# Two attention blocks on one core: N's and h's products alternate, ones product behind M5, sums of v and split of x reordered

## The chip, the cores and the metric

The kernel runs on one core of a Trainium2 chip. The metric is the device time of one execution in microseconds. Before the change it is 2845.95 us, the median of three runs (2843.32, 2845.95 and 2849.13). All data are fp32, in and out.

## What is computed

The input x is eight images of 512 channels and 64 x 64 positions. Two attention layers follow each other; the second one reads what the first one wrote.

```python
# layer 0
f = conv1x1(x, Wf, bf).reshape(b, c // K, h * w)
g = maxpool2x2(conv1x1(x, Wg, bg))
v = maxpool2x2(conv1x1(x, Wh, bh))
s = jnp.einsum('bcn,bcm->bnm', f, g)
beta = jax.nn.softmax(s, axis=-1)
o = jnp.einsum('bcm,bnm->bcn', v, beta).reshape(b, c // 2, h, w)
x = gamma * conv1x1(o, Wv, bv) + x
...
# layer 1
Qf = delu(Q).transpose(0, 2, 1)
Kf = delu(K)
KV = jnp.einsum('bmn,bcn->bmc', Kf, V)
norm = 1.0 / jnp.einsum('bnd,bd->bn', Qf, jnp.sum(Kf, axis=-1) + EPS)
attn = jnp.einsum('bnd,bdc,bn->bcn', Qf, KV, norm)
return x + gamma[0] * attn
```

Q, K and V are 1x1 convolutions of the first layer's result (below "x1"), and delu(x) = 10 relu(x) + exp(10 min(x, 0)).

## The kernel before

**Steps.** An image's 4096 positions are cut into 8 chunks of 512; there are 64 chunks, and `step(s)` (L747) does one chunk's worth of every stage, with the stages shifted against each other. In step s with image b = s // 8 and j = s % 8:

- stage A is for chunk a = s + 9: `a_fg` makes f and g, `a_h` makes h, its pooled form is v. Only 55 of the 64 steps with a chunk of their own (s = 0 to 54) have a stage A.
- E is for chunk s + 1: `weigh_two` makes scores and exponentials E, `sum_of_e` adds them up in r, `total` (L399) sums over partitions with a product by ones, `invert` (L403) takes the reciprocal, `look` (L408) notes two sums that show an overflow, `normalize_block` scales E.
- chunk s itself: `attend` (L437) multiplies v by E in seven products M1 to M7, `project` (L485) multiplies Wv by the result in N1 to N7 and adds it to x, `features` (L549) makes q and k from the new x1.
- chunk s - 1: `split_x`, `turn_halves` and `join_x` (L580 to L596) turn x1 over, `turn_k` turns k, `gather` (L613) makes G = k x1.
- image b - 1: `normalize` and `finish` (pairs of chunks, odd j) make the second layer's attention and add it to the output; `start_kb`, `turn_G` and `make_KV` come at j = 0.

**Seven products.** h, M and N are each a 2x2 block product done with seven products instead of eight. The operands' sums are made beforehand: of x by GpSimd in `sums_of_x` (t1 to t4 into `tha`, `thb`), of v by GpSimd in `sums_of_v` (S1 to S4, once an image), of E by VectorE in `sums_of_e` (T1 to T4), of o by VectorE in `to`. What a product gives is added where it belongs by VectorE. In N it is different: N5, N6 and N3 are accumulated into the PSUM bank of N1, and the bank is evicted between: `evict` (L512) copies it with ScalarE (L517, two instructions) into a scratch tile, and GpSimd adds that to a quarter of x (L520). The order is N1, evict (0,0), N6, evict (1,0), N5, evict (1,1), N3, and what is in the bank then is added by VectorE (`add_rest`, L525, L528). N2, N4 and N7 have banks of their own and are added to x by VectorE (`add`, L523).

**The order.** Nothing is reordered by a scheduler: within a step each piece of work is given a number, `at(t, fn)`, the list is sorted by it (L837), and each engine executes its own instructions in that order. The numbers are meant as microseconds but are no times; a wait is a semaphore between engines. The order of PE's work from N1 on, before the change, is N1 N2 N4 N6 N7 N5 H1 H2 N3 H3 H6 H5 H7 H4, then the turn of v (`a_turn`, pvT), then `features` (pk), then M1 of the next step.

**Buffers.** There are eight PSUM banks of 512 fp32 columns in one pool; `bank()` takes the one that was given back first. x1's chunk (`xb`) has a single buffer: its store, its splits and `features` must be done before the next chunk is loaded. The halves `w0` to `w3` and the turned halves `u0` to `u3` are single too.

**The turn of x1.** `split_x(s, k)` (L583) lets ScalarE part channel block k (128 channels) of x1 into upper and lower 16-bit halves; `turn_halves` turns them by a DMA that SP issues (L589); `join_x` (L596) lets ScalarE put the halves together in `xT`. Channel blocks 0 and 1 are x's quarters (0, .), which N1's last content finishes; blocks 2 and 3 are the quarters (1, .).

SP issues, in order, three transposes, the chunk's store (L534), the fourth transpose, stage A's next load (L200) and the next chunk's load (L205).

Of the kernel before, what the change touches and what calls it, by code (L numbers as in the profile page):

```python
# [38 lines left out]
ALU = mybir.AluOpType  # L39
# [10 lines left out]
def tile_two_attention_blocks(  # L50
# [21 lines left out]
    nc = tc.nc  # L72
# [4 lines left out]
    KT = C // P  # L77
# [86 lines left out]
    def run(ctx, general):  # L164
# [98 lines left out]
        def a_h(a, at, t_sums, t, t_pool):  # L263
            hk = KT // 2

            def sums_of_x():
                b11, b12, b21, b22 = (
                    x_a[a][:, bass.ts(i, hk), bass.ts(j, HN)] for i in range(2) for j in range(2)
                )
                ta, tb = blocks(f"tha_{a}", "T2"), blocks(f"thb_{a}", "T3")  # L270
                t1, t2, t3, t4 = (u[:, bass.ts(i, hk), :] for u in (ta, tb) for i in range(2))
                nc.gpsimd.tensor_tensor(t1, b12, b11, ALU.subtract)  # L272
                nc.gpsimd.tensor_tensor(t2, b22, t1, ALU.subtract)
                nc.gpsimd.tensor_tensor(t3, b22, b12, ALU.subtract)
                nc.gpsimd.tensor_tensor(t4, t2, b21, ALU.subtract)
                th[a] = {1: b11, 2: b21, 3: b22, 4: t4, 5: t1, 6: t2, 7: t3}

            m = {}

            def product(i):  # L280
                m[i] = bank(f"H{i}_{a}")[:, 0:HN]
                for k in range(hk):
                    nc.tensor.matmul(  # L283
                        m[i], w_h7[i][:, k, :], th[a][i][:, k, :], start=(k == 0), stop=(k == hk - 1)
                    )
                if i == 1:
                    u = m["m1"] = scratch(f"h1_{a}")
                    nc.scalar.copy(u[:, 0:HN], m[1])

            def out_1():  # L290
                h = hs[a] = blocks(f"h_{a}", "T4").rearrange("p (v j) n -> p v (j n)", v=VT)
                nc.vector.tensor_tensor(h[:, 0, 0:HN], m["m1"][:, 0:HN], m[2], ALU.add)

            def out_2():
                h, u, w = hs[a], m["m1"], scratch(f"h2_{a}")
                u2, u3 = u[:, HN:CH], w[:, 0:HN]
                nc.vector.tensor_tensor(u2, u[:, 0:HN], m[6], ALU.add)
                nc.vector.tensor_tensor(h[:, 0, HN:CH], u2, m[5], ALU.add)
                nc.vector.tensor_tensor(h[:, 0, HN:CH], h[:, 0, HN:CH], m[3], ALU.add)
                m["u2"], m["u3"] = u2, u3  # L300

            def out_3():
                h, u2, u3 = hs[a], m["u2"], m["u3"]
                nc.vector.tensor_tensor(u3, u2, m[7], ALU.add)
                nc.vector.tensor_tensor(h[:, 1, HN:CH], u3, m[5], ALU.add)
                nc.vector.tensor_tensor(h[:, 1, 0:HN], u3, m[4], ALU.subtract)

            def out_pool():
                vp = vps[a] = work.tile([P, VT, P], F32, tag="vp", name=f"vp_{a}")
                for v in range(VT):  # L310
                    pool(vp[:, v, :], hs[a][:, v, :])

            at(t_sums, sums_of_x)
            for i, d in ((1, -0.9), (2, 0.0), (3, 1.72), (6, 2.58), (5, 3.44), (7, 4.3), (4, 5.16)):
                at(t + d, product, i)
            at(t + 2.6, out_1)
            at(t + 4.4, out_2)
            at(t + 6.1, out_3)
            at(t_pool, out_pool)

        def bias_v(a):
# [11 lines left out]
        def sums_of_v(b):  # L333

            hm = MT // 2
            a11, a12, a21, a22 = (
                st[b]["vT"][:, bass.ts(j, hm), bass.ts(i, P)] for i in range(2) for j in range(2)
            )
            s1, s2, s3, s4 = (
                work1.tile([P, hm, P], F32, tag=f"S{i}", name=f"S{i}_{b}") for i in range(1, 5)  # L340
            )
            nc.gpsimd.tensor_tensor(s1, a21, a22, ALU.add)
            nc.gpsimd.tensor_tensor(s2, s1, a11, ALU.subtract)
            nc.gpsimd.tensor_tensor(s3, a11, a21, ALU.subtract)
            nc.gpsimd.tensor_tensor(s4, a12, s2, ALU.subtract)
            st[b]["v7"] = {1: a11, 2: a12, 3: s4, 4: a22, 5: s1, 6: s2, 7: s3}


# [136 lines left out]
        def project(s, at, t, t_store):  # L485

            m = {}

            def of_x(i, j):
                return x_b[s][:, 2 * i : 2 * i + 2, bass.ts(j, HN)]

            def product(i):
                o, u = os_[s], to[s]
                b = {
                    1: o[:, 0, 0:HN], 2: o[:, 1, 0:HN], 3: o[:, 1, HN:CH],
                    4: u[:, 3], 5: u[:, 0], 6: u[:, 1], 7: u[:, 2],  # L500
                }[i]
                more = i in (6, 5, 3)
                if not more:
                    m[i] = bank(f"N{i}_{s}").rearrange("p (k n) -> p k n", k=2)
                a = m[1] if more else m[i]
                for k in range(2):
                    nc.tensor.matmul(  # L507
                        a[:, k, :], w_v7[i][:, bass.ts(k, P)], b, start=not more and k == 0,
                        stop=True, skip_group_check=more or k > 0,
                    )  # L510

            def evict(ij):  # L512

                u = scratch(f"n{ij[0]}{ij[1]}_{s}").rearrange("p (k n) -> p k n", k=2)
                for k in range(2):
                    c = 2 * ij[0] + k
                    nc.scalar.activation(  # L517
                        u[:, k, :], m[1][:, k, :], AF.Identity, bias=gb_v0[:, c : c + 1]
                    )
                nc.gpsimd.tensor_tensor(of_x(*ij), of_x(*ij), u, ALU.add)  # L520

            def add(ij, i, op):
                nc.vector.tensor_tensor(of_x(*ij), of_x(*ij), m[i], op)  # L523

            def add_rest():  # L525
                for k in range(2):
                    x = x_b[s][:, k, HN:CH]
                    nc.vector.scalar_tensor_tensor(  # L528
                        x, m[1][:, k, :], gb_v0[:, k : k + 1], x, ALU.add, ALU.add
                    )  # L530

            def store():
                b, j = divmod(s, NCHUNK)
                nc.sync.dma_start(out=outr[b, :, :, bass.ts(j, CH)], in_=x_b[s])  # L534

            for n, i in enumerate((1, 2, 4, 6, 7, 5)):
                at(t + 0.86 * n, product, i)
            at(t + 6.88, product, 3)
            at(t + 0.9, evict, (0, 0))
            at(t + 3.45, evict, (1, 0))  # L540
            at(t + 5.2, evict, (1, 1))
            at(t + 3.8, add, (0, 0), 2, ALU.add)
            at(t + 5.6, add, (1, 0), 7, ALU.add)
            at(t + 6.3, add, (1, 0), 4, ALU.subtract)
            at(t + 7.0, add, (1, 1), 7, ALU.add)
            at(t + 7.7, add_rest)
            at(t_store, store)

        def features(s):  # L549
# [39 lines left out]
            nc.sync.dma_start_transpose(out=u, in_=halves[s, k].rearrange("p h n -> p (h n)"))  # L589

        def join_x(s, k):
            if k == 0:
                xTs[s] = turned.tile([P, NT, C], F32, tag="xT", name=f"xT_{s}")
            v = xTs[s].bitcast(U16).rearrange("p t (k c h) -> p k h t c", k=KT, h=2)
            u = turned_halves[s, k].rearrange("p (h t) c -> p h t c", h=2)
            nc.scalar.copy(v[:, k], u)  # L596
# [150 lines left out]
        def step(s):  # L747
# [27 lines left out]
            if 0 <= s - 1 < TOTAL:  # L775
                at(-0.5, features_exp, s - 1)
                at(-0.4, features_sum, s - 1)
                if s < TOTAL:
                    at(-0.45, join_x, s - 1, 1)
                    at(1.8, join_x, s - 1, 2)  # L780
                    at(2.3, join_x, s - 1, 3)
                at(3.6 if here else 0.2, turn_k, s - 1)
                if here:
                    gather(s - 1, at, 12.6, 13.5)
# [14 lines left out]
                finish(pair, (0, 1), at, 9.2)  # L799
                finish(pair, (2, 3), at, 10.9)  # L800
            if 0 <= a < TOTAL:
                a_h(a, at, 19.7, 30.8, 37.8)
                a_fg(a, at, 21.3)
            if 0 <= a - 1 < TOTAL:
                at(18.5, bias_v, a - 1)
# [3 lines left out]
            if after:  # L809
# [2 lines left out]
                at(7.5, weigh_two, n, 2)  # L812
                for m, t in ((2, 9.3), (4, 10.6), (6, 11.8), (8, 13.1)):
                    at(t, sum_of_e, n, m)
                at(16.1, total, n)
                at(17.0, invert, n)
                if not general:
                    at(21.5, look, n)
                at(24.3, normalize_block, n, 0, 1)
                at(26.0, normalize_block, n, 0, 0)  # L820
                at(27.3, normalize_block, n, 1, 1)
# [1 line left out]
                at(33.6, sums_of_e, n, 1)  # L823
                at(36.0, sums_of_e, n, 2)
            if here:
                project(s, at, 24.8, 36.0)
                at(37.0, features, s)
                if s < TOTAL - 1:
                    for k in range(KT):
                        at(32.9 + k, split_x, s, k)  # L830
                        at(33.0 + k, turn_halves, s, k)
                    at(37.3, join_x, s, 0)
                else:
                    for t in range(NT):
                        at(40.4 + t * 0.45, turn_x, s, t)
# [63 lines left out]
```

## Time and profile before

| what | before |
|---|---|
| median of three runs | 2845.95 us |
| the profiled execution, and its span | 2846.64 us, 2844.9 us |
| TensorE's mean granted clock | 0.988 |
| first N product of step 0 starts at | 143.14 us |
| from N1 to the next N1: odd j next, even j next | 43.49 us, 39.95 us (from the second image on) |
| the same where j = 0 leads on to j = 1 | 48.63 us |
| the eight images' part with all stages, 143.1 to 2460.8 | 2317.7 us |
| last eight steps and the end | 384.2 us |

A page describes one execution. PE is TensorE's matmul, PEld its weight load, DVE is VectorE, ACT is ScalarE, POOL is GpSimd, SP issues DMAs. In the list of waits a line reads: engine, tile and line that waited, "<-", the one that released it, then the total in us, the number of times, the longest. In a timeline a line is: start in us, duration in us, engine, line, operation, out<-in, shapes, count, and in brackets the idle time before it and what ended it. In the chain, a line is start, duration and what ran; "issue" is time in which nothing shown was waited for. The end of a matmul is modelled and reaches past the start of the next, so waits of PE are best read from one start to another.

### The profile page before, as it was taken

The numbers are of one execution on the slowest core, as the hardware profiler recorded it, in microseconds if no ns is written. First come the engines' busy times: TensorE is split into PE (matmuls) and PEld (weight loads), VectorE is DVE, ScalarE is ACT, GpSimd is POOL, SyncE is SP. The second block draws the span as 40 slices with busy tenths as digits, with TensorE's granted clock in tenths as the row PEclk, the third lists the DMA queues.
The fourth block names the chain that finished last, engine by engine and source line by source line (L and its number), as shares of the span: only waits on it lengthen the run. The fifth ranks groups of instructions, "written<-read, shape, count | busy, mean of one in ns | idle before, by whom it ended". The sixth has DMA issues, their size and how long they took to land.

```text
span 2844.9 us, 30593 instructions
## 1 busy us (share of the span) xinstructions
PE 2695.6 (95%) x10928; PEld 1810.9 (64%) x10928; DVE 2144.2 (75%) x2982; ACT 1516.6 (53%) x2629; POOL 709.6 (25%) x552
## 2 busy tenths in 40 slices
PE   8899999999999999999999999999999999989984
PEld 6566666666666666666766666666666666655551
DVE  4678778777787777877777877877878777787752
ACT  2255555556556556556556556456555556655542
POOL 4312222222321223222231222322222222211111
PEclk9999999999999999999999999999999999999996
DMA  4143244455454446454455454445544445544456
GB/s 155 36 119 91 88 119 133 97 140 148 115 137 119 108 129 163 98 139 120 118 133 148 106 131 131 120 120 148 118 120 135 118 118 148 133 101 110 112 138 119
DMA packets 394434, 346.96 MB, mean 122 GB/s; under 512 B 274592, under 2 KB 275104, under 8 KB 394272
## 3 DMA queue, kind: packets, MB, share of 16 engines
q1 hardware_dynamic: 371712, 275.82, 34.4%
q0 software_dynamic: 17408, 67.11, 12.7%
q10 hardware_dynamic: 5152, 1.97, 0.3%
q8 instruction: 89, 1.46, 0.2%
q14 instruction: 73, 0.60, 0.1%
HBM read 144.58 MB, written 134.22 MB: 98 GB/s over the span
## 4 chain that ended last, share of the span: by engine, by line
PE 71%; DVE 10%; ACT 8%; issue 4%; DMA 2%; POOL 2%; DVEq 0%; POOLq 0%; ACTq 0%
PE M L444 22%; PE N L507 11%; PE H L283 11%; PE fg L239 7%; PE pk L554 6%; PE s L354 5%; ACT n L517 3%; PE pa L732 3%; DVE r L394 3%; ACT E L358 3%; DMA u<-w 2%; PE tot L401 2%; PE pg L621 2%; DVE r L392 2%; ACT w L583 1%
## 5 line engine op out<-in xcount | busy, mean ns | idle before, releaser
L520 POOL TENSOR_TENSOR xb<-xb,n 128x512 f32<-128x512 f32 x192 | 244.5, 1274 | 596.4 <-ACT n L517 542.9
L444 PEld LDWEIGHTS M<-T,S 128*128 128x128 f32 x1536 | 287.3, 190 | 115.9 <-issue 30.7
L596 ACT COPY xT<-u 128x1024 uint16<-128x1024 uint16 x252 | 336.1, 1343 | 44.3 <-DMA u<-w 42.7
L444 PE MATMUL M<-T,S 128*128 128x256 f32 x1536 | 359.7, 384 | 0.0
L583 ACT COPY w<-xb 128x1024 uint16<-128x1024 uint16 x252 | 244.8, 1042 | 157.3 <-DVE xb L528 157.3
L517 ACT ACTIVATE n<-N,gb_v 128x256 f32<-128x256 f32 x384 | 161.5, 473 | 308.5 <-PE N L507 308.4
L420 DVE TENSOR_TENSOR E<-E,rtot 128x1024 f32<-128x1024 f32 x256 | 304.7, 1213 | 2.4 <-ACT tot L411 1.6
L358 ACT ACTIVATE E<-s 128x512 f32<-128x512 f32 x512 | 257.6, 626 | 42.6 <-PE s L354 42.1
L523 DVE TENSOR_TENSOR xb<-xb,N 128x512 f32<-128x512 f32 x256 | 175.1, 684 | 129.8 <-POOL xb L520 127.5
L507 PE MATMUL N<-to,w_v 128*128 128x256 f32 x1024 | 251.3, 389 | 15.0 <-ACT n L517 10.7
L392 DVE TENSOR_TENSOR r<-E 128x1024 f32<-128x1024 f32 x64 | 78.4, 1225 | 226.6 <-ACT E L358 226.6
L554 PE MATMUL pk<-xb,w_kqk 128*128 128x512 f32 x512 | 235.9, 604 | 10.5 <-DVE xb L528 10.5
L738 POOL DMA_DIRECT2D out_dram<-y x60 | 72.3, 1206 | 678.0 <-ACT y L735 675.8
L354 PE MATMUL s<-f,g 64*128 64x512 f32 x1024 | 239.7, 603 | 0.7 <-ACT kT L611 0.6
L406 DVE RECIPROCAL rtot<-tot 128x512 f32<-128x512 f32 x64 | 215.4, 3365 | 27.6 <-PE tot L401 27.6
L410 ACT ACTIVATE tot<-tot 128x512 f32<-128x512 f32 x64 | 37.2, 582 | 371.6 <-DVE rtot L406 364.5
L507 PEld LDWEIGHTS N<-to,w_v 128*128 128x128 f32 x1024 | 190.0, 191 | 66.5 <-ACT n L517 40.3
L444 PE MATMUL M<-E,vT 128*128 128x256 f32 x1024 | 231.6, 379 | 0.5 <-ACT vT L331 0.5
L272 POOL TENSOR_TENSOR tha<-xa 128x512 f32<-128x512 f32 x58 | 77.0, 1327 | 619.6 <-PE M L444 605.8
L444 PEld LDWEIGHTS M<-E,vT 128*128 128x128 f32 x1024 | 194.5, 190 | 54.0 <-issue 19.8
L507 PE MATMUL N<-o,w_v 128*128 128x256 f32 x768 | 195.1, 390 | 30.2 <-ACT n L517 27.3
L239 PE MATMUL fg<-xa,w_fg 128*128 128x512 f32 x464 | 210.6, 597 | 0.0
(129 smaller groups left out, 4647.0 us busy)
## 6 DMA issues: line engine op xcount, KB each, us to landing
xb<-in_x_dram SPq DMA_DIRECT2D x64, 1024.0 KB, 7.1
out_dram<-xb SPq DMA_DIRECT2D x64, 1024.0 KB, 5.0
out_dram<-y POOLq DMA_DIRECT2D x60, 1024.0 KB, 11.2
xa<-in_x_dram SPq DMA_DIRECT2D x58, 1024.0 KB, 6.6
w_v<-in_L_conv_wv_dram SPq DMA_DIRECT2D x8, 1024.0 KB, 9.1
x_early<-in_x_dram SPq DMA_DIRECT2D x6, 1024.0 KB, 5.4
out_dram<-y_late POOLq DMA_DIRECT2D x4, 1024.0 KB, 17.7
u<-w SPq DMA_TRANSPOSE x252, 3.3
```

The source lines that it names most:

```text
L239: nc.tensor.matmul(fg, w_fg[:, k, :], x_a[a][:, k, :], start=(k == 0), stop=(k == KT - 1))
L283: nc.tensor.matmul(m[i], w_h7[i][:, k, :], th[a][i][:, k, :], start=(k == 0), stop=(k == hk - 1))
L354: nc.tensor.matmul(sc[e], g[half(e), i, :], fs[s][half(e), :], start=True, stop=True)
L358: nc.scalar.activation(es[s][:, 2 * i + e, :], sc[e], AF.Exp)
L420: nc.vector.tensor_tensor(b, b, r, ALU.mult)
L444: nc.tensor.matmul(m[i], v7[i][:, k, :], te[s][i][:, k, :], start=(k == 0), stop=(k == hm - 1))
L507: nc.tensor.matmul(a[:, k, :], w_v7[i][:, bass.ts(k, P)], b, start=not more and k == 0, stop=True, skip_group_check=more or k > 0,)
L517: nc.scalar.activation(u[:, k, :], m[1][:, k, :], AF.Identity, bias=gb_v0[:, c : c + 1])
L520: nc.gpsimd.tensor_tensor(of_x(*ij), of_x(*ij), u, ALU.add)
L554: nc.tensor.matmul(pk, w_kqk[:, i, e * D : (e + 2) * D], x_b[s][:, i, :], start=(i == 0), stop=(i == KT - 1),)
L583: nc.scalar.copy(w, x_b[s][:, k, :].bitcast(U16).rearrange("p (n h) -> p h n", h=2))
L596: nc.scalar.copy(v[:, k], u)
```

## The change

1. In `project` and `a_h` the numbers of the products are set anew: on PE N1 N2 N4 N6 N7 H1 N5 H2 H3 N3 H6 H5 H7 H4. The copy of H1 (`copy_1`, before part of `product(1)`) gets a number of its own and comes behind the eviction (1,1) on ScalarE. The eviction (1,1), VectorE's add of N7 to (1,1), `add_rest` and h's sums get later numbers; their order on VectorE stays.
2. `total` comes behind M5 instead of before it in steps with even j; `invert` comes behind M7's place in all steps. In the one step that has E but no chunk of its own (s = -1), `total` comes behind fg, and `invert` and `look` behind it.
3. GpSimd makes S4 before S3. (M3 needs S4, M7 needs S3.)
4. The channel blocks of x1 are split, turned and joined in the order 2, 3, 0, 1 instead of 0, 1, 2, 3. The last split comes behind `a_turn`'s copy on ScalarE, and the store comes behind the fourth transpose on SP.

```diff
@@ a_h
-                if i == 1:
-                    u = m["m1"] = scratch(f"h1_{a}")
-                    nc.scalar.copy(u[:, 0:HN], m[1])
+
+            def copy_1():
+                u = m["m1"] = scratch(f"h1_{a}")
+                nc.scalar.copy(u[:, 0:HN], m[1])
...
-            for i, d in ((1, -0.9), (2, 0.0), (3, 1.72), (6, 2.58), (5, 3.44), (7, 4.3), (4, 5.16)):
-                at(t + d, product, i)
-            at(t + 2.6, out_1)
-            at(t + 4.4, out_2)
-            at(t + 6.1, out_3)
+            for i, n in ((1, 0), (2, 2), (3, 3), (6, 5), (5, 6), (7, 7), (4, 8)):
+                at(t + 0.86 * n, product, i)
+            at(t + 2.0, copy_1)
+            at(t + 4.45, out_1)
+            at(t + 6.1, out_2)
+            at(t + 7.8, out_3)
@@ sums_of_v
+            nc.gpsimd.tensor_tensor(s4, a12, s2, ALU.subtract)
             nc.gpsimd.tensor_tensor(s3, a11, a21, ALU.subtract)
-            nc.gpsimd.tensor_tensor(s4, a12, s2, ALU.subtract)
@@ project
-            for n, i in enumerate((1, 2, 4, 6, 7, 5)):
+            for i, n in ((1, 0), (2, 1), (4, 2), (6, 3), (7, 4), (5, 6), (3, 9)):
                 at(t + 0.86 * n, product, i)
-            at(t + 6.88, product, 3)
...
-            at(t + 5.2, evict, (1, 1))
+            at(t + 6.05, evict, (1, 1))
...
-            at(t + 7.0, add, (1, 1), 7, ALU.add)
-            at(t + 7.7, add_rest)
+            at(t + 8.2, add, (1, 1), 7, ALU.add)
+            at(t + 8.6, add_rest)
@@ join_x
-            if k == 0:
+            if s not in xTs:
@@ step
-                    at(-0.45, join_x, s - 1, 1)
-                    at(1.8, join_x, s - 1, 2)
-                    at(2.3, join_x, s - 1, 3)
+                    at(-0.45, join_x, s - 1, 3)
+                    at(1.8, join_x, s - 1, 0)
+                    at(2.3, join_x, s - 1, 1)
...
-                a_h(a, at, 19.7, 30.8, 37.8)
+                a_h(a, at, 19.7, 29.1, 37.8)
...
-                at(16.1, total, n)
-                at(17.0, invert, n)
+
+                at((17.85 if j % 2 == 0 else 16.1) if here else 21.4, total, n)
+                at(18.0 if here else 24.2, invert, n)
                 if not general:
-                    at(21.5, look, n)
+                    at(21.5 if here else 24.25, look, n)
...
-                project(s, at, 24.8, 36.0)
+                project(s, at, 24.8, 37.2)
...
-                    for k in range(KT):
-                        at(32.9 + k, split_x, s, k)
-                        at(33.0 + k, turn_halves, s, k)
-                    at(37.3, join_x, s, 0)
+
+                    for i, k in enumerate((2, 3, 0, 1)):
+                        at(33.8 + i, split_x, s, k)
+                        at(33.9 + i, turn_halves, s, k)
+                    at(38.3, join_x, s, 2)
```

## The prediction

> **What bounds the kernel now.** I read the page first (shares and slices), then the list of waits, then one step's timelines on PE, DVE, ACT and SP, then the chain of waits over the same step.
>
> ```profile
> PE 2695.6 (95%) x10928; PEld 1810.9 (64%) x10928; DVE 2144.2 (75%) x2982; ACT 1516.6 (53%) x2629; POOL 709.6 (25%) x552
> ...
> PEclk9999999999999999999999999999999999999996
> ```
>
> TensorE is 95% busy at full clock: it is the bound, and the work given to it does not change. So the change can gain at most TensorE's gaps, about 149 us, and must be judged gap by gap. The waits say what ends them:
>
> ```profile
> PE N L507 <- ACT n L517: 38.0, 70, 1.8
> PE tot L401 <- DVE r L397: 31.0, 37, 4.4
> ...
> PE M L444 <- POOL S L345: 5.6, 8, 3.5
> ```
>
> These three are named by the edits: N behind an eviction, `total` behind the sum of E, M3 behind GpSimd's sums of v. The chain shows the first one inside a step whose N1 starts at 1234.75:
>
> ```profile
> 1234.92 3.47 PE N L507 x16
> ...
> 1238.41 0.85 ACT n L517 x2
> 1239.26 0.04 issue
> 1239.30 1.13 PE N L507 x4
> 1240.43 0.88 PE H L283 x4
> ...
> 1241.60 0.85 ACT n L517 x2
> 1242.45 0.04 issue
> 1242.50 1.13 PE N L507 x4
> 1243.63 4.32 PE H L283 x20
> ```
>
> Read it as: N6 ends, ACT evicts the shared bank, N5 may start; N5 ends, ACT copies h1 and then evicts, N3 may start. Only one product (N7) covers the first eviction; H1 and H2 stand before the second, but H1's own copy goes ahead of it on ACT. The even steps' wait, on PE:
>
> ```profile
> 1306.14 1.99 PE L444 MATMUL M<-T,S 128*128 128x256 f32 x8
> 1308.65 1.10 PE L401 MATMUL tot<-r,ones 128*128 128x512 f32 x2 [0.52 <-DVE r L397]
> ```
>
> **What the Trainium skill says.** PSUM — Partial Sum Buffer, Terms: no two of TensorE, ScalarE and VectorE may access one bank of a partition in the same cycle. So accumulation into N1's bank must stand still while ACT reads it; the trace agrees (N5 starts 0.04 us after the 0.85 us eviction). TensorE: Matmul & The Clock Gate, Part 1: after an idle window of about 3.4 us the array falls to half clock. The trace agrees: after a gap of 4.36 us at 98.8 us, fg took 5.55 us instead of 3.60. GPSIMD Engine Reference, Specifications: GpSimd contends with VectorE instructions that read two SBUF inputs; at 114.3 us a sum of v took 2.36 us beside such work, against 1.26 for its neighbour.
>
> **Part 1, N and h alternate.** A product is four matmuls, 216 ns each (20 in 4.32 us above), so 0.864 us. Nine products from N1 to the end of N3 are 7.78 us; the PE timeline has H3 at 1243.46, 8.71 after N1. Waits: 0.93 us a step. New order: N1 N2 N4 N6 N7 H1 N5 H2 H3 N3 H6 H5 H7 H4. Relative to N1: N6's result could be evicted at 3.66 to 4.50 (as now), N5 comes at 5.18: cover 0.7. N5 ends 6.05; ACT, whose next instruction is now the eviction (h1's copy went behind it), evicts 6.25 to 7.09; N3 comes at 7.78: cover 0.7. Both waits go. The rest of the step: GpSimd's sum of quarter (1,1) 7.2 to 8.45 (1.27 us), DVE's N7 add at 8.5 (now 9.07), add_rest from 9.1 to 10.0 (now 9.7 to 10.6). pk, which needs add_rest, starts at 12.3 (now 13.25), so it has over 2 us. PSUM: each product still finds its bank freed by the same predecessor in issue order: H6 needs N2's add (4.2; H6 at 8.6), H7 needs h1's copy (7.4; H7 at 10.4), pvT and pk need the (1,1) adds: all early. H1 reads x alone, which is loaded. 55 steps have both families; the six with j = 0 after the first image are counted apart: 49 x 0.93 = 45.6 us.
>
> **Part 2, total behind M5 in even steps.** r is ready some 0.55 us after M6 has ended; M5 is 8 matmuls, 1.73 us, and needs only T1. So the wait (M6, begun at 1306.14, issues until 1307.87, tot starts at 1308.65; of these 0.78 a hand-over takes 0.1 anyway, and its second matmul is 0.08 late: 0.75) is covered with 1.0 us to spare. 21 even steps with j > 0 have it: 19 at 0.75, one near 1.0, one at 2.25 of which 0.6 stays: 17 us. Price: the reciprocal (3.37 us) starts as before in time, but PE is one product pair further, so DVE's chain to the normalizing comes up to 1.7 us later against N1: gp's reduce ends at N1 + 2.3, f's copies 3.65, and the (1,0) eviction, queued behind f on ACT, 3.7 to 4.5; N5 needs it at 5.18. The (1,0) adds move to 6.6 to 8.0, still ahead of the (1,1) add at 8.5. Cover 0.5 us; if it is gone each lost 0.1 us costs 2 us in all. Odd steps keep total's place; there pa (3.43 us) covers r already, except s = 1, 3, 5, 7, which keep their wait.
>
> **Part 3, steps with j = 0 (six).** There DVE is late (reciprocal of pd before that of tot), gp's reduce holds f, f holds the eviction, and N5 comes 1.94 us late (N1 at 1144.59 plus five products is 1148.91):
>
> ```profile
> 1150.85 1.13 PE L507 MATMUL N<-to,w_v 128*128 128x256 f32 x4 [1.78 <-ACT n L517]
> ```
>
> That time stays, since DVE's chain hangs on E. But H1 is already done by then, and N3 no longer waits: N5 at 1150.85, then seven products, pvT at 1157.9 instead of 1159.33: 1.46 us. S4 before S3 on GpSimd lets M3 go one sum (1.26 us) earlier; its wait is 0.43: gone, and M7, which now takes the last sum, comes some 15 us later (1256.18 and about 1271.4 in an odd step). 6 x 1.9 = 11.3 us.
>
> **Part 4, x's split.** ACT waits 2.50 us a step for add_rest before split 0. Channel blocks 2 and 3 of x need no add_rest, so split 2 starts at N1 + 9.2 (now 10.2). Split 1 is now behind vT's copy (pvT at 12.1): split 1 12.9 to 13.9, 0.2 earlier than the last split now, while PE is 0.93 earlier. But on SP:
>
> ```profile
> 1289.51 3.99 SPq L589 DMA_TRANSPOSE u<-w  x3
> 1293.59 0.53 SPq L534 DMA_DIRECT2D out_dram<-xb  x1
> 1294.22 1.99 SPq L589 DMA_TRANSPOSE u<-w  x1
> ```
>
> the fourth transpose is issued behind the store and 16.0 after N1; now it goes before it, at 14.5 (first three from 10.25, 1.4 us each, the fourth when split 1 is done). So it lands 1.5 us earlier, or more without the store's 1 MB ahead. Its join, which needed it 0.46 us sooner than it had it, then has room; kT, E and r move with PE. I count nothing, as E is bound by s. The store is issued 0.5 to 1 us later, as are xa's and xb's loads behind it; they have over 10 us (xb's load of 7.1 us is needed 23 us on).
>
> **Part 5, ends.** Before the first real step tot waits 4.36 us and then fg runs at half clock; now fg (3.43) fills that wait. But h's last products then need the banks of look and f, which hang on the reciprocal, so only about 1.5 us arrive at M1; S4's place gives M3 some 2 more (sums of 2.3 us under contention), and M5 before the next tot 1.7 and a shorter half-clock stretch: 6 us, between 3 and 9. In the last eight steps there is no h, N's waits stay; DVE's chain from tot to add_rest bounds even steps, fed by the last transpose, which lands some 1.2 us earlier: 4 us over four steps, between 0 and 8, since half-clock stretches may come or go there.
>
> **Sum**, against the profiled execution (span 2844.9, 2846.64 with what lies around it): 45.6 + 17 + 11.3 + 6 + 4 = 84, so 2762.7; the median shown is 0.7 below that execution: 2762.
>
> **Rivals.**
> Base, 78%: 2745 to 2780.
> A, the E chain does not keep up: split 1 behind vT's copy makes the last transpose late, E follows it instead of s. For: E starts 1.16 after s, with kT just done, in even steps now. Against: 1.5 us gained on SP, and M5 now forgives 1.0. It takes Part 2's 17 us and some of Part 1 in even steps (27 x 0.4): about 2790. 11%.
> B, the alternation does not free N, because ACT or a bank is not free where I think (f before the (1,0) eviction): half of Part 1 and Part 2 lost: 2795 to 2810. 5%.
> C, slower: the same transpose, landing really late. E stays with s while it lands by N1 + 20.8 (join 1.34 and kT 0.36 ahead of E at 22.5), 6.3 us after its issue. What is beyond holds PE in each of 55 steps, less some 1.1 us that M5 and the PSUM banks forgive (pa's first bank is free 1.3 us before pa, at 1260.2 against 1261.54). The gain is 1.5 a step, so C decides from about 9 us after issue; the longest I see is 6.62, at 1209.20 in the chain, behind a store. At 10 us it takes (3.7 - 1.1) x 55 = 143: 2905. 4%. The remaining 2% is no change.
>
> **Numbers.** Base and most of A and B lie in 2744 to 2800. Within 0.2% (5.7 us, about what a measurement of this kernel can tell from none) 2%, slower 4%, faster 94%.
>
> **What would show it.** After: N L507 <- ACT n L517 falls from 38 to some 15 us (j = 0 steps and the last eight), tot's wait from 31 to below 8, M <- POOL S near 0 in the steps; ACT w <- DVE xb shrinks; the step pair falls from 83.4 to about 80.8 us. Wrong, if N5 or N3 still waits in ordinary steps, if DVE's recip-to-gp stretch holds f, or if xT <- DMA u grows on ACT.

## The result, and the profile after

| what | before | after |
|---|---|---|
| median (four runs each) | 2847.52 us | 2773.56 us (2770.26 to 2776.02) |
| ratio, 95% interval | | 0.9742 [0.9725, 0.9759] |
| the profiled execution, and its span | 2846.64, 2844.9 us | 2770.26, 2768.5 us |
| first N product of step 0 | 143.14 us | 136.10 us |
| from there to step 55 | 2317.6 us | 2253.3 us |
| last eight steps and the end | 384.1 us | 379.1 us |

The change makes the kernel 2.6% faster. The span falls by 76.4 us: 7.0 at the start, 64.4 in the steps that have all stages, 5.0 at the end. The forecast had 6, 73.9 and 4. So the steps that have all stages are short by some ten microseconds, and the rest of this document looks for them.

First the page of the kernel after, its shares and its clock:

```profile
PE 2659.8 (96%) x10928; PEld 1820.9 (66%) x10928; DVE 2138.0 (77%) x2982; ACT 1511.6 (55%) x2629; POOL 712.4 (26%) x552
...
PEclk9999999999999999999999999999999999999996
```

The same 10928 matmuls, still at full clock to the eye. The slices of this row are 69 us wide, and that hides something, as will be seen. Then the list of waits on PE, after:

```profile
PE N L509 <- ACT n L519: 21.1, 15, 2.1
...
PE N L509 <- DVE o L476: 9.5, 10, 3.7
...
PE tot L403 <- DVE r L399: 5.7, 6, 2.9
```

The wait behind the eviction was there 70 times and is there 15 times; the wait of `total` was there 37 times and is there 6 times. But the first line is 21.1 us, not the forecast's 15, and its longest entry is 2.1 us where it had been 1.8. One step's PE timeline, in an ordinary even step whose N1 starts at 1197.40, shows what went right:

```profile
1197.40 1.89 PE L509 MATMUL N<-o,w_v 128*128 128x256 f32 x8
1199.13 2.75 PE L509 MATMUL N<-to,w_v 128*128 128x256 f32 x12
1201.72 1.03 PE L283 MATMUL H<-xa,w_h 128*128 128x256 f32 x4
1202.58 1.03 PE L509 MATMUL N<-to,w_v 128*128 128x256 f32 x4
1203.44 1.89 PE L283 MATMUL H<-xa,w_h 128*128 128x256 f32 x8
1205.17 1.03 PE L509 MATMUL N<-o,w_v 128*128 128x256 f32 x4
```

No line has a bracket: N1, N2, then N4, N6 and N7, H1, N5, H2 and H3, N3, without one wait. ScalarE in the same stretch:

```profile
1198.52 0.84 ACT L519 ACTIVATE n<-N,gb_v 128x256 f32<-128x256 f32 x2 [2.94 <-PE N L509]
1199.33 1.38 ACT L257 ACTIVATE f<-fg,b_fg 64x512 f32<-64x512 f32 x2
1201.05 0.84 ACT L519 ACTIVATE n<-N,gb_v 128x256 f32<-128x256 f32 x2 [0.35 <-PE N L509]
1203.64 0.84 ACT L519 ACTIVATE n<-N,gb_v 128x256 f32<-128x256 f32 x2 [1.75 <-PE N L509]
```

The second eviction ends at 1201.89 and N5 starts at 1202.58: 0.69 us of cover (the time by which an eviction is over before PE needs the bank). The third ends at 1204.48, N3 starts at 1205.17: again 0.69. The pair of steps fell from 83.44 to 80.81 us (42.55 + 38.26).

Now a step with j = 0, by engine, after. Three tiles matter: gT, a sum that VectorE makes from the turned G in two instructions; gp, VectorE's pooling of fg; and f, ScalarE's copy of fg, which waits for gp. Behind f in ScalarE's queue stands the eviction (1,0) that N5 waits for. First PE, then VectorE, GpSimd and ScalarE:

```profile
1116.55 1.89 PE L509 MATMUL N<-to,w_v 128*128 128x256 f32 x4 [2.08 <-ACT n L519]
1118.23 2.87 PE L283 MATMUL H<-xa,w_h 128*128 128x256 f32 x8
```

```profile
1103.92 3.36 DVE L408 RECIPROCAL rtot<-tot 128x512 f32<-128x512 f32 x1
...
1110.56 1.82 DVE L672 TENSOR_TENSOR gT<-g 128x256 f32<-128x256 f32 x2
...
1113.54 0.69 DVE L216 TENSOR_REDUCE gp<-fg 64x128 f32<-64x512 f32 x1
```

```profile
1110.44 1.32 POOL L522 TENSOR_TENSOR xb<-xb,n 128x512 f32<-128x512 f32 x1 [4.83 <-ACT n L519]
```

```profile
1114.27 1.38 ACT L257 ACTIVATE f<-fg,b_fg 64x512 f32<-64x512 f32 x2 [3.90 <-DVE gp L216]
```

And the two lines of the kernel before that belong beside them, VectorE's and GpSimd's:

```profile
1145.93 0.75 DVE L671 TENSOR_TENSOR gT<-g 128x256 f32<-128x256 f32 x2
```

```profile
1146.58 1.28 POOL L520 TENSOR_TENSOR xb<-xb,n 128x512 f32<-128x512 f32 x1 [4.83 <-ACT n L517]
```

Before, GpSimd's first addition began 0.1 us before the second gT instruction ended. After, PE reaches N1 earlier against VectorE's chain (N1 stands 4.54 us after the reciprocal of `total` began, before it was 5.29), so the eviction (0,0) and GpSimd's addition come earlier too, and the addition lies on top of gT: 0.75 us becomes 1.82. All of the growth is in the first of the two instructions:

```profile
1110.56 1.49 DVE L672 TENSOR_TENSOR gT<-g 128x256 f32<-128x256 f32 x1
```

It began 0.12 us after GpSimd's addition and was over 0.29 us after it; the second took 0.41 us as before. It is the same in all six j = 0 steps. From the reciprocal to the end of gp's reduction it is now 10.31 us, before it was 9.23. f, the eviction (1,0) and N5 hang on that, one behind the other, and N5 comes 1.08 us later against the reciprocal.

The same two lines of PE show a second loss. H2 and H3, eight matmuls, take 2.87 us where the ordinary step has 1.89, and N5's four take 1.68 from start to start instead of 0.86. Windows over four j = 0 steps (columns: stretch, length, PE busy and count, granted clock, DMA share, GB/s):

```profile
446.50:497.00 50.50, 48.22 (x187) 0.97 0.52 125
778.50:827.00 48.50, 46.23 (x186) 1.00 0.54 130
1108.50:1159.00 50.50, 48.22 (x187) 0.97 0.52 126
1440.00:1490.00 50.00, 47.72 (x192) 1.00 0.53 127
```

In the first and the third of them, and in the one at 1770, the clock fell to half for 3.4 us right behind the wait; in the other three it did not. From N1 to N1 these steps take 50.67 us and 49.00 us by turns, where the kernel before took 48.63.

### The profile page after: what moved, and what is told of

The parts are those of the page before. It is cut to its first block, busy times and chain, and to the rows that moved or that the text cites. A ratio compares the mean times of both kernels' runs of the same rounds, so it can differ in the third digit from the quotient of the medians.

```text
span 2768.5 us, 30622 instructions
## 1 busy us (share of the span) xinstructions
PE 2659.8 (96%) x10928; PEld 1820.9 (66%) x10928; DVE 2138.0 (77%) x2982; ACT 1511.6 (55%) x2629; POOL 712.4 (26%) x552
## 3 DMA queue, kind: packets, MB, share of 16 engines
q10 hardware_dynamic: 5152, 1.97, 0.3%
q8 instruction: 89, 1.46, 0.2%
## 4 chain that ended last, share of the span: by engine, by line
PE 86%; DVE 8%; issue 2%; ACT 2%; POOL 1%; DMA 0%; POOLq 0%; DVEq 0%; ACTq 0%
PE M L446 26%; PE H L283 14%; PE N L509 12%; PE pk L555 8%; PE s L356 7%; PE fg L239 7%; PE pg L622 4%; PE pa L733 3%; PE tot L403 2%; DVE rtot L408 1%; DVE r L396 1%; DVE E L422 1%; PE pkT L610 1%; ACT E L360 1%; PE pkv L686 1%
## 5 line engine op out<-in xcount | busy, mean ns | idle before, releaser
L597 ACT COPY xT<-u 128x1024 uint16<-128x1024 uint16 x252 | 329.3, 1340 | 9.9 <-DMA u<-w 9.0
L584 ACT COPY w<-xb 128x1024 uint16<-128x1024 uint16 x252 | 250.5, 1043 | 118.1 <-DVE xb L525 118.1
L509 PE MATMUL N<-to,w_v 128*128 128x256 f32 x1024 | 248.9, 387 | 15.3 <-ACT n L519 12.5
```

Of the source, the lines that this page charges most:

```text
L509: nc.tensor.matmul(a[:, k, :], w_v7[i][:, bass.ts(k, P)], b, start=not more and k == 0, stop=True, skip_group_check=more or k > 0,)
L584: nc.scalar.copy(w, x_b[s][:, k, :].bitcast(U16).rearrange("p (n h) -> p h n", h=2))
```

## Experiments

The theory: the shortfall sits in the six j = 0 steps. gT is slowed by GpSimd's addition, and the gap that follows sometimes costs the clock. Part 2 (PE ahead of VectorE by the time of M5's move) is what brings the two together. The rivals: Part 1 does not free what it should; the moved copy or the turn of x1 costs; the start gives less than it seems. In the profile of one run the start of step 0 is not a fine gauge: kernels whose start is the same as after's had it at 136.1, 137.95, 137.97 and 138.97 us.

**Part 1 alone.** Before, with the new places of N's and h's products and of h1's copy. The splits keep their old order, only 0.52 later.

```diff
-                    for k in range(KT):
-                        at(32.9 + k, split_x, s, k)
-                        at(33.0 + k, turn_halves, s, k)
+                    for k in range(KT):
+                        at(33.42 + k, split_x, s, k)
+                        at(33.52 + k, turn_halves, s, k)
```

> The alternation of N's and h's products alone, everything else as before. Theory (the waits of N5 and N3 go in 49 steps at 0.93 us; in the six steps with j = 0, N5's wait shrinks by one product, 0.86, and N3's 0.6 goes): 46 + 9 = 55 us, perhaps 3 to 6 of it given back because the last transposed half still comes behind the store and E starts a little late: about 2795, within 2788 to 2803. In the trace the step from N1 to N1 with odd j next falls from 43.49 to 42.55, and no half-clock stretch appears in the steps. Rival (a bank or ACT holds N): under 30 us gained, N5 or N3 still waiting.

Measured: 2804.03 us against 2850.83, ratio 0.9837 [0.982, 0.9853]. The ordinary steps fell by 0.94 each, and all six j = 0 steps from 48.63 to 47.17 us, by the 1.46 that the forecast had for them. gT stayed at 415 ns. So neither the alternation nor its count is what failed. The rest of the expectation was missed: 2804.03 against about 2795, above its range of 2788 to 2803. The profiled execution, 2810.53, is the longest of the four; in it five steps waited 2.09 to 2.23 us for `total`, where the kernel before has one such wait (2.09 us, at 1225.21 us), and behind three of the five the clock fell to half, which was not expected either. PE at one of them:

```profile
619.97 1.10 PE L403 MATMUL tot<-r,ones 128*128 128x512 f32 x2 [2.23 <-DVE r L399]
620.91 5.30 PE L446 MATMUL M<-T,S 128*128 128x256 f32 x16
```

The sixteen matmuls behind the gap take 3.62 us at full clock; here a part of them ran at half. ScalarE's fourth join had waited for its transpose:

```profile
610.71 1.34 ACT L597 COPY xT<-u 128x1024 uint16<-128x1024 uint16 x1 [1.74 <-DMA u<-w]
```

That transpose was issued at 604.81, behind the store. In all five steps the fourth join had waited so, by 1.19 to 1.74 us. With the old turn of x1 the late fourth transpose can come onto the path. That the faster steps are the reason why it does so more often is argued from one trace of each kernel, and not shown.

**Part 2 alone.**

```diff
-                at(16.1, total, n)
-                at(17.0, invert, n)
+                at(17.85 if here and j % 2 == 0 else 16.1, total, n)
+                at(18.0 if here else 17.0, invert, n)
```

> total behind M5 in even steps and invert behind M7, alone, and only in steps with a chunk of their own. My prediction's sum: 17 us from 21 even steps, 2 at s = 0, j = 0 unchanged: 2829. Theory formed from the changed kernel's trace: in j = 0 steps the VectorE chain is what N5 waits for, PE comes 0.75 us earlier to the eviction (0,0), so GpSimd's add of that quarter runs beside the sum gT, which reads two SBUF inputs: gT grows from 0.75 to some 1.8 us, N5's wait grows to about 3.8 us and most of these steps get a half-clock stretch of 3.4 us: 6 x (1.07 + up to 1.7) = 6 to 16 us back. So 2835 to 2843.

Measured: 2847.25 us against 2850.83, 0.998 [0.9969, 0.9991], above the expected 2835 to 2843. The eleven executions spread from 2837.97 to 2850.02 us; the fastest has a mean granted clock of 0.987, the slowest 0.982. The profiled one, 2842.79, is one of the faster ones. In its trace the even steps fell from 39.95 to 39.20, the 0.75 that was counted. And yet next to nothing is left of 17 us in the median. Every j = 0 step grew: from 48.63 to 50.46 us in two of them and to between 51.55 and 52.77 in four, where the clock fell. 50.46 is 48.63 + 0.75 + 1.08: what the step ahead of it gained is given back, since VectorE's chain has not moved, and gT is slow. The last eight steps lose another 3.9 us (388.0 instead of 384.1). The group of gT in this kernel (count, then busy us and mean ns):

```profile
L671 DVE TENSOR_TENSOR gT<-g 128x256 f32<-128x256 f32 x16 | 12.4, 816 | 0.0
```

Before, the mean was 415 ns. So the loss in the j = 0 steps belongs to Part 2, not to Part 1.

**Parts 3 and 4 of the change alone** (S4 before S3; the splits in the order 2, 3, 0, 1 and the store behind the fourth transpose).

```diff
-            nc.gpsimd.tensor_tensor(s3, a11, a21, ALU.subtract)
             nc.gpsimd.tensor_tensor(s4, a12, s2, ALU.subtract)
+            nc.gpsimd.tensor_tensor(s3, a11, a21, ALU.subtract)
...
-                project(s, at, 24.8, 36.0)
+                project(s, at, 24.8, 37.2)
...
-                    for k in range(KT):
-                        at(32.9 + k, split_x, s, k)
-                        at(33.0 + k, turn_halves, s, k)
+                    for i, k in enumerate((2, 3, 0, 1)):
+                        at(33.8 + i, split_x, s, k)
+                        at(33.9 + i, turn_halves, s, k)
```

> S4 before S3 and the order 2, 3, 0, 1 of the splits with the store behind the fourth transpose, nothing else. Theory: 7 waits of M3 at 0.43 us (3), about 2 us at the first sums of v, about 1.7 us in the one step whose total waits 2.09 for a late transpose, 4 to 5 us in the last eight steps: 8 to 13 us, 2835 to 2840. If the splits' order were worth more (every step's ACT wait of 2.5 us for add_rest), it would be tens of us; if ACT's last split behind vT's copy hurt, slower than before.

Measured: 2835.7 us against 2850.83, 0.9948 [0.9932, 0.9965]. M3's wait is gone from the steps (the step from j = 7 to j = 0 went from 41.79 to 41.25), no wait for `total` is as long as the 2.09 us that the kernel before has at 1225.21 us, ScalarE's joins wait 7.8 us for transposes instead of 42.7, and the last eight steps with the end took 379.8 us instead of 384.1.

**The copy alone.** Before, with nothing but h1's copy behind the eviction (1,1).

```diff
-                if i == 1:
-                    u = m["m1"] = scratch(f"h1_{a}")
-                    nc.scalar.copy(u[:, 0:HN], m[1])
+
+            def copy_1():
+                u = m["m1"] = scratch(f"h1_{a}")
+                nc.scalar.copy(u[:, 0:HN], m[1])
...
+            at(t - 0.75, copy_1)
```

> The kernel before with one instruction moved: h1's copy behind the eviction (1,1) on ScalarE, products in the old order. If N3's wait is the copy standing before the eviction: the eviction starts 0.2 us after N5, ends 1.05 after it, N3 comes 1.73 after it, so N3's wait of 0.61 goes in 55 steps, 33 us: 2814; N5's 0.33 stays. Rival (N3 waits for the eviction's length whatever stands before it): no change, 2847.

Measured: 2811.5 us against 2850.83, 0.9867 [0.985, 0.9885]. PE in an even step:

```profile
1219.44 3.95 PE L509 MATMUL N<-to,w_v 128*128 128x256 f32 x16
1223.23 1.89 PE L283 MATMUL H<-xa,w_h 128*128 128x256 f32 x8
1224.95 1.03 PE L509 MATMUL N<-o,w_v 128*128 128x256 f32 x4
```

N3 at 1224.95 follows H2 without a wait. The sixteen matmuls of N4, N6, N7 and N5 take 3.79 us from start to start where 16 x 0.216 is 3.46, so N5's 0.33 us is still there. A step gains 0.61 of the 0.94. (A wait of 2.09 us for `total` is in this trace too, at 619.68 us.) Most of Part 1 was ScalarE's order, not PE's: a copy of 0.38 us, which itself needs H1, stood ahead of an eviction that PE was waiting for.

**The copy put back.** After, with the copy ahead of the eviction again.

```diff
-            at(t + 2.0, copy_1)
+            at(t + 1.7, copy_1)
```

> The changed kernel with h1's copy ahead of the eviction (1,1) again, products alternating. If the alternation by itself takes the copy out of N3's way (H1 ends 0.9 us before N5, so the copy of 0.37 us is over when the eviction may start): no change from the changed kernel, 0.974 of before, steps still 38.26 and 42.55 us. If the copy's place is what carries the gain: 33 us lost, 0.986.

Measured: 2772.51 us against 2849.59, 0.9739 [0.9724, 0.9754], with steps of 38.26 and 42.55 as after has them. With two products of h between N5 and N3 the copy fits in front. Either edit removes N3's wait; on that wait they do not add.

**The turn of x1 undone.** After, with part 4 of the change as it was before.

```diff
-                    for i, k in enumerate((2, 3, 0, 1)):
-                        at(33.8 + i, split_x, s, k)
-                        at(33.9 + i, turn_halves, s, k)
-                    at(38.3, join_x, s, 2)
+                    for k in range(KT):
+                        at(33.42 + k, split_x, s, k)
+                        at(33.52 + k, turn_halves, s, k)
+                    at(37.3, join_x, s, 0)
```

> The changed kernel with the splits of x1 in the old order 0, 1, 2, 3 and the store before the fourth transpose. My prediction counts nothing for that part in full steps and 4 us in the last eight: 0.976 of before. Theory from the run with the alternation alone: there two even steps waited 2.2 us for r behind a late fourth transpose; with M5 ahead of total only some 0.6 us of such a wait would remain, so 2 to 4 us in all, and 5 us at the end: 0.976 to 0.978. If the part carries more, total waits again in many steps, 0.98 and above.

Measured: 2785.6 us against 2846.18, 0.9784 [0.9769, 0.9799]; after has 0.9742, so part 4 is worth about 0.4%, some 12 us, a little more than expected. The profiled execution (2788.74) is the longest of the four and 18.5 us longer than that of after: 3.8 at the start, 6.3 in the full steps and 8.4 in the last eight (387.5 us). Of the 6.3, 1.7 is one more j = 0 step at half clock, and 2.1 are waits for `total` that came back or grew (0.36 to 0.93 us in seven steps); ScalarE's joins wait 64.9 us for transposes, in after 9.0. This is SP's queue in after:

```profile
1250.21 5.36 SPq L590 DMA_TRANSPOSE u<-w  x4
1255.66 0.53 SPq L536 DMA_DIRECT2D out_dram<-xb  x1
```

Four transposes in a row, then the store. Whether the order of the splits or the place of the store does more was not separated.

**gT out of the way.** After, with VectorE's gT behind h's first sums in the six j = 0 steps.

```diff
-            at(t + 1.5, out)
+            at(33.58 if t > 20 else t + 1.5, out)
```

> The changed kernel with VectorE's two sums gT moved from before the normalizing to behind h's first sum, where GpSimd is idle, in the six steps with j = 0. Theory (gT, grown from 0.83 to 1.82 us by GpSimd's add beside it, stands before gp, f and the eviction that N5 waits for): gT back at 415 ns, N5's wait falls by 1.8 from 2.24 us to about 0.4, and the half-clock stretches of three of these steps go: 6 x 1.8 + 3 x 1.7 = 16 us, 0.9685 of before. Rival (f and the eviction hang on the reciprocals' chain alone): N5's wait stays above 1.2, under 5 us.

Measured: 2761.86 us against 2846.18, 0.9702 [0.9687, 0.9717]. PE and VectorE in the j = 0 step at 1105:

```profile
1111.47 1.13 PE L509 MATMUL N<-to,w_v 128*128 128x256 f32 x4 [0.33 <-ACT n L519]
```

```profile
1116.59 0.75 DVE L672 TENSOR_TENSOR gT<-g 128x256 f32<-128x256 f32 x2
```

gT takes 0.75 us again, N5 waits 0.33 instead of 2.08, all six steps take 47.24 or 47.25 us, and in none of them does the clock fall. The full steps gain 15.6 us and take 2237.7; the forecast's count for them was 2317.6 - 73.9 = 2243.7, which still had gT's 0.75 us on the chain six times. The end gives 4.9 back: there the product that uses gT waits 2.39 us, which it did not do in after, and its eight matmuls then take 6.59 us, where the eight of pk behind them take 3.43. With gT off the chain, the missing time is there. (This run takes out the whole of gT, 1.82 us; that 1.07 of it is the meeting with GpSimd is read from the traces of before, after and Part 2 alone.)

**Less work ahead of the chain.** After, with the reciprocal of the second layer's norm (3.36 us on VectorE) moved up in the j = 0 steps.

```diff
-                normalize(pair, at, 5.6, 13.2)
+                normalize(pair, at, 5.6, 9.25)
```

> The changed kernel with VectorE's reciprocal of pd and its product (3.35 + 0.69 us) moved, in steps with j = 0, from behind the sums r to before them, where VectorE waits some 3.2 us for E. Theory: r comes up to 0.9 us later, which M5 hides (1.0); the reciprocal of tot comes right after tot, so o, gp and f are early, N2, N4 and N5 no longer wait (0.36 + 0.2 + 2.24 + 0.3 us), no half-clock stretch, gT at 415 ns: 6 x 3.0 + 3 x 1.4 = 22 us, 0.9665 of before. Rival: r's delay is not covered and total waits as long as N5 did: 0.974, as the changed kernel.

Measured: 2749.01 us against 2846.18, 0.9655 [0.9642, 0.9668]. VectorE in the j = 0 step whose N1 is at 1105.05:

```profile
1087.09 3.36 DVE L708 RECIPROCAL rn<-pd 128x512 f32<-128x512 f32 x1
...
1097.93 3.37 DVE L408 RECIPROCAL rtot<-tot 128x512 f32<-128x512 f32 x1 [0.35 <-PE tot L403]
...
1104.56 0.75 DVE L672 TENSOR_TENSOR gT<-g 128x256 f32<-128x256 f32 x2
```

The reciprocal of `total` now waits for PE instead of standing behind the other one; gT is done at 1105.31, before N1's bank has been evicted. N no longer waits, and the j = 0 steps take 45.98 us. `total` waits 0.59 us in front of them, so the step ahead takes 40.40 instead of 39.58; the two together gain 2.2 us, and 3.9 where the clock had fallen. So even the part of this wait that the kernel before had was a matter of order on VectorE.

**That, and `total` behind M5 in the first image's odd steps as well.**

```diff
-                normalize(pair, at, 5.6, 13.2)
+                normalize(pair, at, 5.6, 9.25)
...
-                at((17.85 if j % 2 == 0 else 16.1) if here else 21.4, total, n)
+                at((17.85 if j % 2 == 0 or not c_here else 16.1) if here else 21.4, total, n)
```

> As the run before, and total behind M5 in the odd steps of the first image too (no pa stands there before total). Four waits of 0.75 us go: 3 us below the run before, 0.9655 of before.

Measured: 2745.45 us against 2846.18, 0.9642 [0.9629, 0.9655]. The first image's remaining steps of 39.01 us become 38.26, and the fastest of the kernels tried is this one, a percent below after. The two intervals overlap, but all five times of this run (2742.63 to 2745.91) lie below all five of the run above (2746.10 to 2751.28), and the steps show where.

**The start put back.** After, with `total`, `invert` and `look` of step -1 where they were.

```diff
-                at((17.85 if j % 2 == 0 else 16.1) if here else 21.4, total, n)
-                at(18.0 if here else 24.2, invert, n)
+                at(17.85 if here and j % 2 == 0 else 16.1, total, n)
+                at(18.0 if here else 17.0, invert, n)
...
-                    at(21.5 if here else 24.25, look, n)
+                    at(21.5, look, n)
```

> The changed kernel with total, invert and look of step -1 where they were. My prediction gives that step's reordering some 1.5 us of the 6 at the start. The changed kernel's first N starts at 136.10 us against 143.14; the run with total alone has 139.88 and that with the small edits 142.30, so up to 3 us may be this: N1 of step 0 at 138 to 140 us, 0.974 to 0.9755 of before.

Measured: 2772.01 us against 2849.59, 0.9732 [0.9718, 0.9745]. In this trace the first N product comes at 137.41 us, 1.3 later than in after, but that is within what kernels with one and the same start differ by. The expected 138 to 140 us and 0.974 to 0.9755 were missed: no loss is seen. The two intervals overlap and are 8 and 10 us wide, so what fg's place is worth here stays open.

## Why the prediction was right, and where it was not

The forecast was 2762 us with a range of 2744 to 2800; 2773.56 lies inside, and in the base case (2745 to 2780). That it came so near is in part luck: a loss of 11.5 us that the forecast did not have was offset by some 4 us of gains that it did not have either.

**Part 1** was right in mechanism and size. N5 came at N1 + 5.18 and N3 at N1 + 7.77 (forecast 5.18 and 7.78), with the 0.7 us of cover given for each, and a step gained 0.94 (forecast 0.93). What the forecast did not see is how little of this needed PE's order: h1's copy alone gave 0.61.

**Part 2** was right in the ordinary even steps: 0.75 us each, the (1,0) eviction at N1 + 3.65 to 4.49 (forecast 3.7 to 4.5), no wait at N5. The first image's odd-numbered waits of 0.52 stayed, as said.

**Part 3 is the step that failed.** "That time stays, since DVE's chain hangs on E" counted the j = 0 steps as 1.46 us shorter. As Part 2 lets PE run 0.75 us ahead, the chain from reciprocal to f does not stay: GpSimd's addition moves onto gT, and the chain grows by 1.08 us. 49.00 is 48.63 - 1.46 + 0.75 + 1.08, of which the 0.75 only moved in from the step ahead. In three of six steps the clock takes another 1.67; how many they are can't be told from the kernel alone (four in the trace with the turn of x1 undone; the last section has what picks them). Together 6 x 1.08 + 3 x 1.67 = 11.5 us; from 73.9 that leaves 62.4, and 64.4 was measured. The other 2 us are made up of small gains that the forecast had put lower (the 0.6 us that was to stay of the longest of these waits is gone, and M3's wait was worth 0.54 instead of 0.43 in six steps). Part 2 did price the case in which its cover is gone, but worked it out for ordinary even steps only; for j = 0, where the cover was already less than nothing, it was never asked what else would move. The forecast had even quoted the price: the Trainium skill, GPSIMD Engine Reference, Specifications, says that GpSimd contends with VectorE instructions that read two SBUF inputs, and a sum of v had shown 2.36 against 1.26 us. It was applied to the start and not to gT, which has the same kind of inputs. This trace agrees with the page: the sum of gT that met the addition took 1.49 us, the one that did not 0.41.

M3's wait went, as forecast: two of 0.5 us are left, at the start and in the last steps.

**Part 4** was counted at nothing in the full steps ("I count nothing, as E is bound by s"). In the sum as it stands that is no error, as E does follow s in after; but it is a condition for the rest. Undone, it costs about 12 us, and Part 1 without it shows waits of 2.23 us for `total`. Rival A expected part 4 to make the last transpose late and `total` to wait; it was the other way round: such waits come back, small, when part 4 is undone. The long landing that rival C needed never came: ScalarE's waits for transposes fell from 42.7 to 9.0 us, where the forecast feared that they might grow.

**Part 5** came out as 7.0 and 5.0 against 6 and 4, where the 7.0 lies at the upper end: with the starts of the other traces it would be 4.2 to 7.1. H4 waiting for the reciprocal's banks is there as foreseen (2.34 us at 107.67). The last eight steps gained by part 4, as the run of it alone and the run without it show.

**Rival B** has its mechanism, f before the (1,0) eviction, in the j = 0 steps only. One sign that the forecast named appeared there: VectorE's stretch to gp holds f. Of the 21.1 us in PE's list, 12.5 are these six waits of 2.08 us, and 8.6 lie in the last eight steps and the end.

## What to carry to other kernels

When one engine is made earlier against another, list for each place where they meet what will now run at the same time, and price what two engines cost each other when they run together, as well as waits; a step type that was already late deserves its own sum. An edit that removes a wait on PE may be done more cheaply on the queue of the engine that PE waits for: look first at what stands ahead of the awaited instruction there. An edit counted at nothing can still be the condition under which the others pay, so it is tested by undoing it from the full change as well as by doing it alone.

## What the hardware showed that was not expected

- A VectorE sum of two SBUF inputs, 128x256 fp32, took 1.49 us instead of 0.41 when it began 0.12 us after a GpSimd addition of 128x512, and was over only 0.29 us after that addition. The mean of all sixteen gT sums, 817 ns against 415, hides that six took 1.49 us and ten 0.41 or 0.42. GpSimd's own instruction hardly changed (1.28 to 1.32 us). At 114.3 us of the kernel before, where the two began within 0.01 us of each other, it was GpSimd's sum that took longer (2.36 us instead of 1.26) and VectorE's sum of 128x1024 that took its usual 1.22.
- TensorE fell to half clock for 3.4 us behind a gap of about 2.1 us before N5, in three of six steps that show the same gap. The Trainium skill, TensorE: Matmul & The Clock Gate, Part 1, names an idle window of about 3.4 us (3413 ns), running free of the kernel. The length of the slow stretch agrees; the gap was shorter than the window, so here the measurement decides: 2.1 us can be enough, and 1.78 us, in the kernel before, was not in any of its six steps.
- The traces tell, as far as these steps go, what picks the three. The slow stretches of after end at 458.01, 1120.20 and 1782.38 us, 662.19 and 662.18 us apart, which is 194 windows of 3413 ns: this grid runs on through the whole kernel, as the page says. In the three slow steps one window of the grid holds the whole gap (2.24 us from start to start, less the 0.216 of a matmul); in the other three a window ends inside the gap, and the fullest holds 1.52, 1.74 and 1.97 us. The ends of the slow stretches fix the grid in the same way in four more traces (Part 2 alone, the copy put back, the turn undone, the start put back). In the thirty j = 0 steps of the five, the clock fell in all 17 where one window held 2.21 us of idle time or more, and in none of the 13 where the fullest held 2.15 us or less. This is no limit for other gaps: of the five waits for `total` in Part 1 alone, the clock fell in two where one window held 2.27 and 2.39 us, but also in one where the fullest held 2.01, and not in two with 2.00 and 2.01. A clock row in slices of 69 us does not show these stretches; windows of one step do.
